# Seven pairs of states per half summed by accumulating DMAs, with a new order of the work

## The chip, the core and the metric

The kernel runs on one core of a Trainium2 chip. The metric is device time in microseconds (us). The engines are TensorE (PE in the profile, its weight loads PEld), VectorE (DVE), ScalarE (ACT), GpSimd (POOL) and SyncE (SP, which here only issues DMAs).

## The reference, cut to what matters

The input is 4096 rows of 1024 numbers in fp32. Three blocks follow each other, each added to the rows: half of a linear layer with ternary weights on the normalised rows, a selective state-space layer, and the linear layer again. Only the middle one matters for the change:

```python
xz = x @ W_in.T;  u, z = split(xz)                 # 2 x 1024 channels
u  = silu(conv_b + sum(conv_w[:, k] * shifted u))  # 4 taps
dt = softplus(dt_r @ W_dt.T + b_dt)                # dt_r, B, C = u @ W_xproj.T
h  = exp(dt * A) * h + dt * B_t * u                # 16 states n per channel, in order of t
y  = sum over n of h[n] * C_t[n] + u * Dskip
out = (y * silu(z)) @ W_out.T
```

The sum in the line of `y` has seventeen terms: one for each of the sixteen states, and the term with `Dskip`.

## The kernel before

**Tiling.** The rows are cut into 16 chunks of 256 rows. In the state-space layer the 1024 channels of a chunk are two halves of 512, so there are 32 halves. A tile of a half is 128 partitions by 4 blocks by 256 rows, 512 KB in fp32.

**One state of one half.** Five streams work on state `n`, from -1 (the `Dskip` term) and 0 to 15.
- `decaying` (ACT, line 911) makes the decays `da`, four instructions.
- `enter` (POOL, lines 934 and 944) makes `h = g * B` in two instructions, and adds what the chunk before left.
- `recur` (DVE, line 969) runs the recurrence in two scans, and `left` (DVE, line 985) multiplies by C: the *product* `p`.
- `summed` (PE, line 1052) transposes a product with the identity into the two PSUM accumulators `y`, eight matrix instructions for a product. That is how the seventeen terms are added up.
- `skipping` (ACT, line 897) makes the term -1.

The product tiles have five buffers, `h` three, the broadcast rows `bc` of B and C six, and the streamed weights five.

**Pairs.** Two terms can be added before PE sees them, so that PE transposes their sum alone. `PAIRED` names states whose product DVE adds to that of the state before (`paired`, line 1002). `SENT` names states for which POOL issues a DMA that accumulates the earlier product onto the later one, both in SBUF (`beside`, line 1020); its source's buffer comes free when it has landed. Before, `SENT` is (1, 5, 9) in every half. `PAIRED` is (7,) in the 28 halves of chunks 1 to 14, (12, 14) in the two halves of the first chunk, and empty in the last. So PE transposes 13, 12 and 14 products in a half of the middle chunks, the first and the last.

**Other work.** Around the states run the linear layers (`ffn`, line 488, with `normed`, `transposed`, and `cut` at 445 and 447, and an accumulating DMA of the bias from DRAM, line 461), the input projection of u (`front`, line 608, and `conv`, 539 to 549), of z (`gates`, line 668, and `kept`, 682 to 687) and the output projection (`back`, line 751, and `mixed`, 722). They stream their weights with DMAs issued by SP (`streamed`), 512 KB each.

**What sets the order.** The instructions of each engine run in an order fixed when the program is built. The class `Streams` holds a clock for each engine and reckons, from durations written into the streams, which stream comes next; constants give the ranks of the streams (`DECAY` to `FFN_C`, `Z`), how long a lower rank is held back for a higher one (`HOLD`), margins on when something counts as ready (`LATE_P` for a product, `LATE_D` for a decay, `LATE_N` and `LATE_X`), and at which recurrence step a piece of the other work may begin (`TRIG`). A DMA of a pair counts as landed `ISSUE` (600 ns) and `ADDED` (9500 ns) after its issue begins, and its transposes may begin 160 ns (`REACH`) later. On the chip only semaphores decide when an instruction may start; the order stays. In `summing` the sum of a pair that goes by DMA is put 3.2 states later in PE's order (`DEFER`).

Of the kernel before, what the change touches and what calls it, by code (L numbers as in the profile page):

```python
# [27 lines left out]

FULL, PASS, TURN = 0.844, 0.449, 0.855
REACH = 160  # L30
ISSUE, ADDED = 600, 9500
SWITCH = 1300

LATE_P, LATE_X, LATE_D, LATE_N = 400, 100, 1700, 1300
PAIRED = (7,)
PAIRED_FIRST = (12, 14)
PAIRED_LAST = ()
TRIG = (-11, -16, 5, 1, -6, -16, 16, -2, 9, 12, 0, -17, 7, -7, -19, -8, -12)
ENTERED = 2
POOLED = ()  # L40
SENT = (1, 5, 9)
DEFER = 2.2, 3.2
Q_SOON = False

DECAY, ENTER, SUM, PREPARE, RECUR, GATE = 5, 0, 0, 0, 4, 1
FFN_A, NORM, U_PART, CONV, DELTA, OUT, FFN_C = 0, 5, 1, 3, 4, 2, 1

HOLD = (1300, 0, 100, 2600)
Z = (5, 7)


class Streams:
# [109 lines left out]
def macaron_mamba_kernel(  # L162
# [169 lines left out]

    def streamed(load, n, ahead, rank):

        queue = []

        def fill():
            for i in range(n):
                yield lambda: 0 if len(queue) < ahead else INF
                w = yield from weights.take()  # L340
                load(i, w)
                queue.append((order.now + 5000, w))

        order.spawn(fill(), rank)
        return queue

    def arrived(queue):
        yield lambda: queue[0][0] if queue else INF
        return queue.pop(0)[1]

    def u_weights(i, w):
# [76 lines left out]
            order.spawn(parts(g, pt, end + REACH), rank)  # L428


    def ffn(c, which, rank, at, tiles=range(TT)):
        ln, rows_, at = yield from stats(c, at, tiles)
        key = which, c

        def split(t):

            xn, begin = yield from normed(c, ln, rows_, t, at)
            hi = yield from his.take()
            lo = yield from los.take()
            ends = []  # L440

            def cut(g, pt, at_):
                part_hi, part_lo = (flat(p_[:, 4 * g : 4 * g + 4, :]) for p_ in (hi, lo))
                end = yield act(512, at_)
                nc.scalar.copy(part_hi, pt)  # L445
                end = yield dve(600, end + REACH)
                nc.vector.tensor_tensor(part_lo, pt, part_hi, ALU.subtract)  # L447
                banks.put(pt, end)
                ends.append(end)
                if len(ends) == NB // 4:  # L450
                    ready["parts", key, t] = end + REACH + LATE_N
                    parts[t] = lo, hi

            order.spawn(biased(t, begin), rank)
            yield from transposed(xn, begin, cut, rank)

        def biased(t, at_):

            yield from when("hbias")
            end = yield pool(ISSUE, at_, False)  # L460
            nc.gpsimd.dma_start(x_tiles[c, t], hbias.to_broadcast([P, D]), accum_op=ALU.add)
            ready["bias", key, t] = end + ADDED

        def residual(t, cols, pf, at_):
            at_ = max(at_, (yield from when("bias", key, t)))
            end = yield dve(660, at_)
            xt = x_tiles[c, t][:, cols]
            nc.vector.scalar_tensor_tensor(xt, pf, hscl, xt, ALU.mult, ALU.add)  # L468
            (ys if (*key, t) == ("a", 0, 1) else banks).put(pf, end)
            ready["ffn", key, t, cols.start] = end  # L470
            if key == ("c", NC - 1):
                yield from give_out(c, t, cols, end)

        parts = {}
        for t in tiles:
            order.spawn(split(t), rank)
        if key == ("a", 0):
            yield from as_weights_come(key, parts, residual, rank)
        for t in tiles if key != ("a", 0) else ():
            begin = yield from when("parts", key, t)  # L480
            lo, hi = parts[t]
            for h in range(2):
                cols = slice(h * OH, (h + 1) * OH)
                pf = yield from banks.take()
                for x in (lo, hi):
                    end = yield pe(8 * OH * PASS, 0, "r")
                    for k in range(NB):
                        nc.tensor.matmul(  # L488
                            pf,
                            x[:, k, :],  # L490
                            wf[:, k, cols],
                            start=(x is lo and k == 0),
                            stop=(x is hi and k == NB - 1),
                        )
                order.spawn(residual(t, cols, pf, end + REACH + LATE_X), rank)
            los.put(lo, end)
            his.put(hi, end)
        lns.put(ln, end if key != ("a", 0) else order.now)
        ends = {}
        for t in tiles:  # L500
            left = yield from when("ffn", key, t, 0)
            right = yield from when("ffn", key, t, OH)
            ends[t] = max(left, right)
        return ends

    def as_weights_come(key, parts, residual, rank):

        for t in range(TT):
            yield from when("parts", key, t)
        groups = {}  # L510
        for h in range(2):
            groups[0, h] = yield from banks.take()
            groups[1, h] = yield from ys.take()
        for k in range(NB):
            yield from when("wf", k)
            end = yield pe(8 * OH * PASS, 0, "r")
            for (t, h), pf in groups.items():
                for i in range(2):
                    nc.tensor.matmul(
                        pf,  # L520
                        parts[t][i][:, k, :],
                        wf[:, k, h * OH : (h + 1) * OH],
                        start=(k == 0 and i == 0),
                        stop=(k == NB - 1 and i == 1),
                    )
        for (t, h), pf in groups.items():
            order.spawn(residual(t, slice(h * OH, (h + 1) * OH), pf, end + REACH), rank)
        for t in range(TT):
            los.put(parts[t][0], end)
            his.put(parts[t][1], end)  # L530
# [4 lines left out]
    def conv(c, blk, pp, at):  # L535
        half, b = divmod(blk, HB)
        ub, rows_ = u[c, half][:, b, :], pp[:, KER - 1 : KER - 1 + T]
        end = yield act(T, at)
        nc.scalar.activation(  # L539
            ub,  # L540
            rows_,
            AF.Identity,
            bias=pr[:, blk, C_CB : C_CB + 1],
            scale=pr[:, blk, C_CW + KER - 1 : C_CW + KER],
        )
        for k in range(KER - 1):
            end = yield dve(391, end + (REACH if k == 0 else 111))
            tap = pr[:, blk, C_CW + k : C_CW + k + 1]
            nc.vector.scalar_tensor_tensor(ub, pp[:, k : k + T], tap, ub, ALU.mult, ALU.add)  # L549
        banks.put(pp, end)  # L550
        done = ready.setdefault(("conv", c, half), [])
        done.append(end)
        if len(done) == HB:
            end = yield act(D, end + REACH, "silu")
            nc.scalar.activation(flat(u[c, half]), flat(u[c, half]), AF.Silu)
            ready["u", c, half] = end + REACH

    def front():
        for c in range(NC):
# [28 lines left out]
            for t in range(TT):  # L588
                xn, at = xns[t]
                yield from transposed(xn, at, keep, NORM)  # L590
                while len(ends) < 2 * (t + 1):
                    yield lambda: ends[2 * t + 1] if len(ends) > 2 * t + 1 else INF

            end = yield pool(190)
            nc.gpsimd.tensor_copy(xT[:, :, PAD - KER + 1 : PAD], halo)  # L595
            at = max(end, ends[-1]) + REACH
            yield U_PART
            for blk in range(NB):
                yield from step(c, 2 + blk // 2)
                if blk % HB == 0:  # L600
                    u[c, blk // HB] = yield from us.take()
                pp = yield from banks.take()
                w = yield from arrived(queue)
                wt = w.rearrange("p (k m) -> p k m", m=P)
# [75 lines left out]
    def kept(c, half, b, pp, at):  # L680
        end = yield act(512, at)
        nc.scalar.copy(sz[c, half][:, :, b * P : (b + 2) * P], pp)
        banks.put(flat(pp), end)
        if b + 2 == HB:
            z = flat(sz[c, half])
            end = yield act(D, end + 125, "silu")
            nc.scalar.activation(z, z, AF.Silu)
            ready["z", c, half] = end + REACH

# [37 lines left out]
    def turned(c, half, yT):  # L727
# [15 lines left out]
                nc.tensor.transpose(pt[:, cols], sz[c, half][:, t, cols], ident)  # L743
            order.spawn(keep(t, pt, end + REACH), OUT)
        szs.put(sz[c, half], end)
        yield lambda: ends[-1] if len(ends) == TT else INF

    def by_w_out(po, yT, w, half, t):
        wt = w.rearrange("p (k m) -> p k m", m=QW)
# [207 lines left out]
    def recur():  # L957
        behind = None
        for c, half, n in items:
# [4 lines left out]
            for j in range(2):  # L964
# [3 lines left out]
                rows_ = flat(h[:, 2 * j : 2 * j + 2, :])  # L968
                nc.vector.tensor_tensor_scan(rows_, flat(da), rows_, 0.0, ALU.mult, ALU.add)  # L969
                decays.put(da, end)  # L970
                ready["step", (2 * c + half) * NST + n] = end
                if behind and j == 0:
                    yield from left(*behind)
                if behind and j == (0 if Q_SOON else 1):
# [38 lines left out]
    def beside(c, half, n):  # L1013
# [4 lines left out]
        if n in SENT:  # L1018
            end = yield pool(ISSUE, at, False)
            nc.gpsimd.dma_start(flat(p), flat(q), accum_op=ALU.add)  # L1020
            end = end + ADDED
        else:
            for j in range(0, HB, 2):
                end = yield pool(1250, at, True)
# [128 lines left out]
```

## Time and profile before

| | us |
|---|---|
| median of 3 runs (2601.02 to 2603.2) | 2602.99 |
| the profiled execution | 2601.62 |
| its span, first to last instruction | 2599.9 |
| PE busy | 2441.9 (94%) |
| PE weight loads busy | 2093.8 (81%) |
| DVE busy | 2314.4 (89%) |
| ACT busy | 1925.1 (74%) |
| POOL busy | 1896.4 (73%) |

A busy time is the sum of one engine's instructions in the profiled execution. Matrix instructions overlap each other, so PE's time per instruction is better read from the distance between starts. The DMA queues are told apart by who builds the transfers: q1 carries what SP issues, q0 what POOL issues (96 pairs and 64 biases).

### The profile page before, as it was taken

The page shows a single profiled execution, that of the slowest core. Times are in us where ns is not written, and L with a number is a line of the kernel's source. Part 1 is how long each engine was busy: PE and PEld are TensorE (multiplying, and loading weights), DVE is VectorE, ACT ScalarE, POOL GpSimd, SP SyncE. Part 2 cuts the span into 40 slices and gives each one's busy share as a digit, 9 for nine tenths or more (in the row PEclk, how much of TensorE's full clock was granted, in tenths as well). Part 3 has the DMA queues.
Part 4 walks back from the last instruction along what each step waited for, and adds up shares of the span by engine and source line. Part 5 has one row for each costly group of instructions (what it writes and reads, how often), then busy time and mean ns, then how long its engine had stood idle before and what let it go on. Part 6 is the DMA issues. An engine that isn't in the chain of part 4 may idle for free. (4 is left out here: it accounts for less than half of the span.)

```text
span 2599.9 us, 39031 instructions
## 1 busy us (share of the span) xinstructions
PE 2441.9 (94%) x13058; PEld 2093.8 (81%) x13058; DVE 2314.4 (89%) x2468; ACT 1925.1 (74%) x4056; POOL 1896.4 (73%) x2041
## 2 busy tenths in 40 slices
PE   5988899999999999999999999999999999999787
PEld 4776787888888888888888888888888888887676
DVE  4588998999999899999989999899999989999795
ACT  3678677687877868787786868878687786877563
POOL 0467867778787787878778686877878677787683
PEclk9989999999999999999999999999999999999888
DMA  4546556766766666666566765665675567666462
GB/s 165 156 129 187 175 158 178 198 180 195 197 173 166 196 185 199 186 182 188 167 190 195 203 178 161 189 195 168 196 207 168 167 193 191 188 192 173 149 165 65
DMA packets 232369, 461.03 MB, mean 177 GB/s; under 512 B 20708, under 2 KB 87396, under 8 KB 232168
## 3 DMA queue, kind: packets, MB, share of 16 engines
q1 hardware_dynamic: 209128, 374.65, 43.2%
q0 software_dynamic: 23040, 83.90, 18.6%
q8 instruction: 103, 1.69, 0.3%
q14 instruction: 98, 0.80, 0.1%
HBM read 390.82 MB, written 17.31 MB: 157 GB/s over the span
## 5 line engine op out<-in xcount | busy, mean ns | idle before, releaser
L934 POOL TENSOR_TENSOR h<-u,bc 128x512 f32<-128x512 f32 x1024 | 1339.5, 1335 | 444.9 <-ACT da L911 153.2
L969 DVE TENSOR_TENSOR_SCAN h<-da,h 128x512 f32<-128x512 f32 x1024 | 1215.4, 1206 | 78.8 <-ACT da L911 54.9
L911 ACT ACTIVATE da<-dt,pr 128x255 f32<-128x255 f32 x2048 | 953.1, 474 | 409.2 <-DVE h L969 373.7
L985 DVE TENSOR_TENSOR p<-h,bc 128x1024 f32<-128x1024 f32 x512 | 672.5, 1314 | 0.1
L1052 PE MATMUL y<-ident,p 128*128 128x128 f32 x3328 | 438.5, 278 | 69.0 <-DVE p L985 35.0
L668 PE MATMUL bank<-weight,xT 128*128 128x256 f32 x2048 | 479.5, 383 | 14.5 <-DMA weight<-in_w_in 9.6
L608 PE MATMUL bank<-xT,weight 128*128 128x259 f32 x2048 | 475.4, 385 | 14.3 <-POOL xT L595 5.2
L1052 PEld LDWEIGHTS y<-ident,p 128*128 128x128 f32 x3328 | 387.0, 143 | 124.1 <-DVE p L985 48.5
L751 PE MATMUL bank<-weight,u 128*128 128x256 f32 x2016 | 452.6, 381 | 7.7 <-DMA weight<-in_w_out 7.1
L608 PEld LDWEIGHTS bank<-xT,weight 128*128 128x128 f32 x2048 | 382.1, 191 | 77.3 <-issue 8.9
L668 PEld LDWEIGHTS bank<-weight,xT 128*128 128x128 f32 x2048 | 378.6, 192 | 65.9 <-ACT da L911 9.8
L751 PEld LDWEIGHTS bank<-weight,u 128*128 128x128 f32 x2016 | 381.4, 191 | 60.4 <-issue 5.6
L944 POOL TENSOR_TENSOR h<-h,over 128x4 f32<-128x4 f32 x512 | 272.0, 531 | 36.1
L488 PE MATMUL bank<-wf,lo 128*128 128x512 f32 x976 | 258.3, 407 | 5.3 <-DVE lo L447 3.8
L488 PE MATMUL bank<-wf,hi 128*128 128x512 f32 x976 | 243.3, 391 | 0.0
L488 PEld LDWEIGHTS bank<-wf,lo 128*128 128x128 f32 x976 | 181.5, 191 | 49.7 <-DVE x L468 7.6
L549 DVE SCALAR_TENSOR_TENSOR u<-bank,pr,u 128x256 f32<-128x256 f32 x384 | 176.8, 469 | 43.4 <-ACT u L539 40.9
L488 PEld LDWEIGHTS bank<-wf,hi 128*128 128x128 f32 x976 | 182.8, 189 | 37.6
L417 PE MATMUL bank<-ident,tmp 128*128 128x128 f32 x756 | 116.0, 288 | 38.1 <-ACT tmp L401 26.6
L386 ACT ACTIVATE tmp<-x,ln 128x1024 f32<-128x1024 f32 x96 | 110.1, 1146 | 37.8 <-POOL ln L384 37.6
L417 PEld LDWEIGHTS bank<-ident,tmp 128*128 128x128 f32 x756 | 95.5, 149 | 51.6 <-ACT tmp L401 28.8
L468 DVE SCALAR_TENSOR_TENSOR x<-bank,hscl,x 128x512 f32<-128x512 f32 x124 | 91.6, 739 | 43.4 <-PE bank L488 41.9
(99 smaller groups left out, 1936.2 us busy)
## 6 DMA issues: line engine op xcount, KB each, us to landing
bc<-bcd SPq DMA_DIRECT2D x512, 256.0 KB, 4.1
weight<-in_w_in SPq DMA_DIRECT2D x128, 512.0 KB, 4.8
weight<-in_w_in SPq DMA_DIRECT2D x256, 256.0 KB, 5.3
weight<-in_w_out SPq DMA_DIRECT2D x128, 512.0 KB, 6.1
p<-p POOLq DMA_DIRECT2D x96, 512.0 KB, 5.8
x<-hbias POOLq DMA_DIRECT2D x64, 512.0 KB, 8.1
x<-in_x SPq DMA_DIRECT2D x32, 512.0 KB, 4.7
out<-x SPq DMA_DIRECT2D x30, 512.0 KB, 4.7
```

The source lines that it names most:

```text
L417: nc.tensor.matmul(pt[:, j * P : (j + 1) * P], xn[:, k * P : (k + 1) * P], ident, start=(j == 0), stop=(j == 3), is_transpose=True, skip_g ...
L488: nc.tensor.matmul(pf, x[:, k, :], wf[:, k, cols], start=(x is lo and k == 0), stop=(x is hi and k == NB - 1),)
L549: nc.vector.scalar_tensor_tensor(ub, pp[:, k : k + T], tap, ub, ALU.mult, ALU.add)
L608: nc.tensor.matmul(pp[:, : KER - 1 + T], wt[:, k, :], xT[:, k, PAD - KER + 1 : PAD + T], start=(k == 0), stop=(k == NB - 1),)
L668: nc.tensor.matmul(pp[:, t, :], xT[:, k, PAD + t * P : PAD + (t + 1) * P], wt[:, :, i, :], start=(k == 0 and t == 0), stop=(k == NB - 1), ...
L751: nc.tensor.matmul(po[:, t, :], yT[:, b, t * P : (t + 1) * P], wt[:, b, :], start=(half == 0 and t == 0 and b == 0), stop=(half == 1 and b ...
L911: nc.scalar.activation(da[:, i, 1:], dt[c, half][:, b, 1:], AF.Exp, scale=a_neg[:, half * HB + b, n : n + 1],)
L934: nc.gpsimd.tensor_tensor(h[:, some, :], u[c, half][:, some, :], bc[:, 0:1, :].to_broadcast([P, ENTERED, T]), ALU.mult,)
L944: nc.gpsimd.tensor_tensor(h[:, :, 0], h[:, :, 0], over[c, half][:, :, n], ALU.add)
L969: nc.vector.tensor_tensor_scan(rows_, flat(da), rows_, 0.0, ALU.mult, ALU.add)
L985: nc.vector.tensor_tensor(p, h, bc[:, 1:2, :].to_broadcast([P, HB, T]), ALU.mult)
L1052: nc.tensor.matmul(y[t][:, b * P : (b + 1) * P], p[:, b, t * P : (t + 1) * P], ident, start=(first and b == 0), stop=(final and b == HB - ...
```

## The change

`SENT` becomes (0, 2, 4, 6, 8, 10, 12) in every half, and the three `PAIRED` lists become empty. So in each half the terms (-1, 0), (1, 2) to (11, 12) are added by seven accumulating DMAs, and PE transposes ten tiles: seven sums, and the products 13, 14 and 15. A pair's DMA counts as landed `SUMMED` (7500 ns) after the issue, in place of 9500. Several waits of the reckoning name the stage that they need (each part of `cut`, each block of `conv`, each part of `kept`), where they counted stages done. A recurrence step counts as done for `TRIG` after its second scan, no longer after its first. The ranks, margins and triggers have other values. No other instruction of the engines is added or taken away.

```diff
-ISSUE, ADDED = 600, 9500
+ISSUE, ADDED, SUMMED = 600, 9500, 7500
-LATE_P, LATE_X, LATE_D, LATE_N = 400, 100, 1700, 1300
-PAIRED = (7,)
-PAIRED_FIRST = (12, 14)
+LATE_P, LATE_X, LATE_D, LATE_N = 1600, 300, 0, 900
+PAIRED = ()
+PAIRED_FIRST = ()
 PAIRED_LAST = ()
-TRIG = (-11, -16, 5, 1, -6, -16, 16, -2, 9, 12, 0, -17, 7, -7, -19, -8, -12)
+TRIG = (-7, -26, -11, 12, -9, 17, -9, -24, -1, 37, -40, -9, -4, -1, -2, -14, 44)
-SENT = (1, 5, 9)
+SENT = (0, 2, 4, 6, 8, 10, 12)
-DECAY, ENTER, SUM, PREPARE, RECUR, GATE = 5, 0, 0, 0, 4, 1
-FFN_A, NORM, U_PART, CONV, DELTA, OUT, FFN_C = 0, 5, 1, 3, 4, 2, 1
-HOLD = (1300, 0, 100, 2600)
-Z = (5, 7)
+DECAY, ENTER, SUM, PREPARE, RECUR, GATE = 9, 4, 6, 1, 9, 6
+FFN_A, NORM, U_PART, CONV, DELTA, OUT, FFN_C = 0, 7, 3, 1, 0, 7, 5
+HOLD = (500, 100, 100, 0)
+Z = (8, 7)
...
     def streamed(load, n, ahead, rank):
-        queue = []
+        queue, gone = [], []
         def fill():
             for i in range(n):
-                yield lambda: 0 if len(queue) < ahead else INF
+                if i >= ahead:
+                    yield lambda: gone[i - ahead] if len(gone) > i - ahead else INF
...
+    def cuts(key, t):
+        for g in range(NB // 4):
+            yield from when("cut", key, t, g)
...
-                ends.append(end)
-                if len(ends) == NB // 4:
-                    ready["parts", key, t] = end + REACH + LATE_N
-                    parts[t] = lo, hi
+                ready["cut", key, t, g] = end + REACH + LATE_N
...
-        done = ready.setdefault(("conv", c, half), [])
-        done.append(end)
-        if len(done) == HB:
-            end = yield act(D, end + REACH, "silu")
-            nc.scalar.activation(flat(u[c, half]), flat(u[c, half]), AF.Silu)
-            ready["u", c, half] = end + REACH
+        ready["conv", c, blk] = end + REACH
+    def activated(c, half):
+        for blk in range(half * HB, (half + 1) * HB):
+            end = yield from when("conv", c, blk)
+        end = yield act(D, end, "silu")
+        nc.scalar.activation(flat(u[c, half]), flat(u[c, half]), AF.Silu)
+        ready["u", c, half] = end + REACH
...
-                ready["step", (2 * c + half) * NST + n] = end
+                if j:
+                    ready["step", (2 * c + half) * NST + n] = end
...
             nc.gpsimd.dma_start(flat(p), flat(q), accum_op=ALU.add)
-            end = end + ADDED
+            end = end + SUMMED
```

More of the change, by code (lines that the diff above doesn't have):

```diff
@@ L344, in streamed @@
         order.spawn(fill(), rank)
-        return queue
+        return queue, gone
     def arrived(queue):
-        yield lambda: queue[0][0] if queue else INF
+        queue, gone = queue
+        at = yield lambda: queue[0][0] if queue else INF
+        gone.append(at)
         return queue.pop(0)[1]
@@ L439, in split @@
             lo = yield from los.take()
-            ends = []
+            parts[t] = lo, hi
             def cut(g, pt, at_):
@@ L479, in ffn @@
         for t in tiles if key != ("a", 0) else ():
-            begin = yield from when("parts", key, t)
+            yield from cuts(key, t)
             lo, hi = parts[t]
@@ L508, in as_weights_come @@
         for t in range(TT):
-            yield from when("parts", key, t)
+            yield from cuts(key, t)
         groups = {}
@@ L590, in front @@
                 yield from transposed(xn, at, keep, NORM)
-                while len(ends) < 2 * (t + 1):
-                    yield lambda: ends[2 * t + 1] if len(ends) > 2 * t + 1 else INF
+                yield lambda: max(ends) if len(ends) == NB // 4 * (t + 1) else INF
             end = yield pool(190)
             nc.gpsimd.tensor_copy(xT[:, :, PAD - KER + 1 : PAD], halo)
-            at = max(end, ends[-1]) + REACH
+            at = max(end, max(ends)) + REACH
             yield U_PART
@@ L601, in front @@
                     u[c, blk // HB] = yield from us.take()
+                    order.spawn(activated(c, blk // HB), CONV)
                 pp = yield from banks.take()
@@ L683, in kept @@
         banks.put(flat(pp), end)
+        ready["kept", c, half, b] = end + 125
         if b + 2 == HB:
+            for b in range(0, HB, 2):
+                end = yield from when("kept", c, half, b)
             z = flat(sz[c, half])
-            end = yield act(D, end + 125, "silu")
+            end = yield act(D, end, "silu")
             nc.scalar.activation(z, z, AF.Silu)
@@ L745, in turned @@
         szs.put(sz[c, half], end)
-        yield lambda: ends[-1] if len(ends) == TT else INF
+        yield lambda: max(ends) if len(ends) == TT else INF
     def by_w_out(po, yT, w, half, t):
```

## The prediction, made before the change had been run

> **What bounds the kernel now.** I read the page's busy times first, then the stages, to see whether those shares hold throughout.
>
> ```profile
> PE 2441.9 (94%) x13058; PEld 2093.8 (81%) x13058; DVE 2314.4 (89%) x2468; ACT 1925.1 (74%) x4056; POOL 1896.4 (73%) x2041
> ```
>
> ```profile
> core 0: us, PE busy (x) PEld busy (x) DVE busy (x) ACT busy (x) POOL busy (x), PEclk, DMA share, GB/s
> 0.00:130.00 130.00, 97.27 (x430) 80.21 (x431) 66.35 (x93) 64.74 (x114) 34.54 (x54) 0.93 0.51 161
> 610.00:930.00 320.00, 312.97 (x1704) 269.68 (x1704) 298.12 (x318) 246.23 (x523) 251.38 (x265) 1.00 0.66 188
> 2500.00:2600.00 100.00, 80.27 (x392) 66.78 (x390) 67.61 (x68) 38.46 (x89) 49.21 (x52) 0.89 0.45 123
> ```
>
> The middle of the run, 290 to 2210 us, looks like the second stage: PE 98% busy, DVE 93%, ACT 77%, POOL 79%. Only the ends have much empty PE time. Chunks follow each other every 151 us: the sixteen halo copies of line 595 start from 48.3 to 2312.1, (2312.1 - 48.3) / 15 = 150.9, so a half takes 75.5 us. Ends of matrix instructions are modelled, so I checked PE's load by starts in the timeline:
>
> ```profile
> 1268.97 1.04 PE L1052 MATMUL y<-ident,p 128*128 128x128 f32 x8
> 1269.85 3.62 PE L668 MATMUL bank<-weight,xT 128*128 128x256 f32 x16
> 1273.30 1.04 PE L608 MATMUL bank<-xT,weight 128*128 128x259 f32 x4
> ```
>
> The eight transposes of a product are busy for 1.04 us but hold PE for 0.88 (to the next start); the sixteen of L668 hold it 3.45, or 0.216 each. In such distances, the three projections (6144 instructions, 0.216) hold PE 1327 us, the linear layers (2048, about 0.24 each: 8 of L488 busy 1.98 to 2.19 us) some 490, transposes (4352, 0.11) 479, the small products (512, 0.216) 111: together 2407 of 2600. So PE is nearly full by either measure, and is the bound; DVE is second, close behind.
>
> The Trainium skill (Perfetto Trace Analysis, Identifying the Most-Contended Engine) says that matmul busy time judges TensorE's headroom badly and weight-load busy time well. By that rule PE stands at 81%, DVE at 89% is the most contended, and the gain would be at most DVE's 53.7 us below, about 2549. The start distances speak for the matmul row here.
>
> **The change part by part.** The rows that price it:
>
> ```profile
> L969 DVE TENSOR_TENSOR_SCAN h<-da,h 128x512 f32<-128x512 f32 x1024 | 1215.4, 1206 | 78.8 <-ACT da L911 54.9
> ...
> L668 PE MATMUL bank<-weight,xT 128*128 128x256 f32 x2048 | 479.5, 383 | 14.5 <-DMA weight<-in_w_in 9.6
> ...
> L751 PE MATMUL bank<-weight,u 128*128 128x256 f32 x2016 | 452.6, 381 | 7.7 <-DMA weight<-in_w_out 7.1
> L1052 PE MATMUL y<-ident,p 128*128 128x128 f32 x3328 | 438.5, 278 | 69.0 <-DVE p L985 35.0
> ...
> L1002 DVE TENSOR_TENSOR p<-p,p 128x1024 f32<-128x1024 f32 x32 | 53.7, 1678 | 0.0
> ...
> q0 software_dynamic: 23040, 83.90, 18.6%
> ...
> p<-p POOLq DMA_DIRECT2D x96, 512.0 KB, 5.8
> ```
>
> ```profile
> L1020 POOL DMA_DIRECT2D p<-p x96: 860/881/948, 119.0 to 2539.3; - x96
> DMA to landing us min/median/max: 4.6/5.8/10.7
> ```
>
> ```profile
> PE y L1052 <- DVE p L1002: 23.6, 16, 5.0
> ...
> DVE h L969 <- POOL h L944: 23.9, 27, 3.1
> ```
>
> (A group's line ends with its idle time and what ended it; the last fence holds waits: us in total, times, longest; the one before, all issues of a pair's transfer and its landings.)
>
> *PE loses transposes.* 3328 / 8 = 416 products now; ten in each of 32 halves after, 320. The 96 fewer are three in each of 28 middle halves, two in each of the first two, four in each of the last two. At 0.88 us they free 84 us. The 12 of the first and last chunk (11 us) lie in the stages where PE is 75 to 80% busy; I count them at nothing, as other waits end last there. The 84 products of the middle lie where PE is full: 84 x 0.88, -74 us. Bounds: -84, and nothing if DVE or a transfer takes over.
>
> *DVE loses 32 adds*, 53.7 us. They free nothing more while PE is the bound. But DVE must keep up. In the 1920 us of the middle lie about 25 halves: DVE falls from 1780 to 1780 - 25 x 1.68 = 1738, PE from 1869 to 1869 - 76 x 0.88 = 1802; at PE's present fill the stretch would last 1851 us, with DVE's empty time down from 140 to 113. If all the 27 us of lost slack become waits of PE, it costs 27; if none, nothing. I take 10: the largest waits of DVE are for PE and ACT (ACT da 54.9, PE bank L488 41.9), not DVE holding PE up.
>
> *POOL gets 128 more issues*, 128 x 0.891 = 114 us, or 3.6 us in each half. POOL is empty for some 16 of a half's 75.5 us (79% busy), so they fit. What is queued behind an issue is `enter` of the next state, and behind that DVE's scan. Today DVE waits for POOL's `h` 27 times in 1024 scans, 23.9 us in all. Bounds: nothing, and 114 us if every issue delays a scan. I take 5, near the row.
>
> *The wait moves from an add to a landing.* PE waits today 23.6 us for the adds of L1002, which go. In PE's queue 224 sums, not 96, then stand behind a landing, and everything PE does is queued behind them. In the list of waits no line has PE waiting for a `p` transfer. The order allows 600 + 7500 + 160 = 8.26 us from issue to transposes (10.26 before); the median landing is 5.8, the longest 10.7. Bounds: -24 us; and 2.4 us (10.7 - 8.26) for one in ten of 224, +54, less 24, so +30. I take 0, since the median is well inside.
>
> *The DMA engines.* 160 transfers of q0 take 18.6% of 2600 us, 3.0 us each over all sixteen engines. 128 more add 387 us, taking q0 to q14 together from 62% to 77%. Weights are what they can hold up: PE waits 9.6 + 7.1 = 16.7 us for them now (L668 and L751). A pair's transfer is in flight 96 x 5.8 / 2600 = 21% of the time, afterwards 224 x 5.8 / 2555 = 51%; scaled with that the waits become 40 us. Bounds 0 and +23; I take 12, as not all of today's waits come from pairs.
>
> The skill's SBUF page (SBUF — State Buffer, SBUF: two separate sides) speaks against sending by POOL: DVE instructions that hold the port shared with GpSimd keep it from writing descriptors. If every added issue waited for one product of 1.2 us, that would be 154 us, on the landings. The row of issues, 860 to 948 ns, shows no such wait in the instruction itself, though the landings spread by 6 us.
>
> *The buffers.* A state takes 75.5 / 16 = 4.7 us. With 8 us from issue to landing, the earlier product stays some 15 us and the later some 13, every 9.4 us: three buffers of five on average. No cost.
>
> *The new order.* No row prices it. In the middle PE waits for 2% of the time, about 45 us over the run, and that is all a better order can win; for a loss, the second stage above (312.97 of 320 us) against the least full one of the middle, 290 to 610 us (309.15), differs by 3.8 in 320, 31 over a run. So -45 to +31, taken as 0. The named waits change what the reckoning knows, and no instruction.
>
> **The sum.** -74 + 10 + 5 + 0 + 12 = -47 us. On the profiled execution: 2601.6 - 47 = 2554.6; the median of the runs is 1.4 higher: 2556.
>
> **The rivals.**
> - *Landings come late, and PE's queue stands.* Place: the 224 sums in PE's order. An accumulating transfer needs all engines for 3.0 us; with 77% of their time taken, one more transfer ahead of it makes a usual landing 5.8 + 3.0 = 8.8 us, 0.54 beyond what the order allows. Price: 224 x 0.54 = 121 us if it hits all, 60 if it hits half. It decides from 47 / 224 = 0.21 us of mean lateness. For it: transfers in flight half of the time, an allowance cut by 2 us, landings up to 10.7 already. Against it: no PE wait for 96 of them today. With half of them: 2556 + 60 = 2616.
> - *DVE becomes the bound.* Its 93% leaves only 5.5 us in a half; if order and port keep it there, the middle shrinks only by DVE's 42 us less POOL's delays and the weights' (5 + 12): -25, about 2578. For it: the busy shares lie close. Against it: DVE's waits are mostly for PE's banks, which come earlier.
> - *All of it comes through.* PE's 84 us and the 24 us of waits for adds, DMA and POOL hidden: 2603 - 108 = 2495. For it: POOL and the DMA engines have room. Against it: the ends of the run do not shrink with PE.
> - *The pairs do not come about.* Then PE would still transpose 416 products and the time would be 2603, but for the order. `summing` and `beside` read `SENT` alone, so I see little chance.
>
> **How the numbers follow.** A measurement of this kernel can tell about 0.2%, 5 us, from no change. Chances: the forecast (2525 to 2570) 0.45; DVE as the bound (2570 to 2597) 0.18; all of it (below 2525) 0.12; late landings or an order that loses as much (above 2608) 0.20; no pairs, or gain and loss equal (2598 to 2608) 0.05. So faster 0.75, same 0.05, slower 0.20. The range reaches from 2512, within the third case, to 2625, just beyond half of the landings being late; I leave about 0.08 below and 0.10 above. The likeliest sign's own range is 2512 to 2597.
>
> **What would show it.** The page after should have 2560 transposes at L1052's successor, about 100 us less busy there (96 x 1.04); no DVE add of `p<-p`; 224 issues of `p<-p`, 200 us; DMA busy near 77%. If the forecast holds, chunks come every 148 us, the middle keeps PE at 97% and DVE near 94%, and the median landing stays below 7 us. Late landings would show as PE (or PEld) `y` waiting for DMA `p<-p`, by more than 47 us in all, with PE below 95%. DVE as the bound would show DVE above 95% in the middle and PE waiting for DVE. I am wrong in kind if PE's empty time in the middle grows by more than the 74 us that it lost in work.

## The result, and the profile after

The changed kernel takes 2620.5 us (median of 4 runs, 2619.3 to 2621.7) against 2603.1 before: 1.0069 times as long, 95% interval 1.0051 to 1.0086. The prediction was 2556, faster. Its profiled run is 2619.6 us, span 2617.8.

First the page of the changed kernel: busy times, the group of the z projection (line 674, before 668), the transposes, and the pairs' issues.

```profile
PE 2384.6 (91%) x12290; PEld 2036.1 (78%) x12290; DVE 2297.3 (88%) x2436; ACT 1910.2 (73%) x4055; POOL 1997.0 (76%) x2169
...
q0 software_dynamic: 41472, 151.01, 31.7%
...
L674 PE MATMUL bank<-weight,xT 128*128 128x256 f32 x2048 | 505.9, 400 | 87.7 <-DMA weight<-in_w_in 84.4
...
L1062 PE MATMUL y<-ident,p 128*128 128x128 f32 x2560 | 331.2, 278 | 32.3 <-DMA p<-p 22.0
...
L1030 POOL DMA_DIRECT2D p<-p x224 | 202.7, 905 | 15.9 <-issue 11.5
...
p<-p POOLq DMA_DIRECT2D x224, 512.0 KB, 6.2
```

Everything that was meant to go has gone: 768 transposes less (107 us of busy time), no add on DVE, 224 issues. Yet PE is busy for a smaller share of a longer span, and one line has grown: waits for the z weights, from 9.6 to 84.4 us. The list of waits has its count, and a second wait that was 5.8 us before (ACT for rows of x):

```profile
PE bank L674 <- DMA weight<-in_w_in: 84.4, 16, 7.3
...
ACT tmp L385 <- DMA x<-in_x: 47.3, 15, 4.0
```

Of the sixteen waits, fourteen are 5.4 to 7.3 us long, one in each of fourteen chunks. Here is the one near 1165 us, on PE and then on SP, the queue that issues the weights (start, length, instruction, idle time before it in brackets):

```profile
1156.13 5.45 PE L674 MATMUL bank<-weight,xT 128*128 128x256 f32 x24
1161.42 1.04 PE L1062 MATMUL y<-ident,p 128*128 128x128 f32 x8
1162.29 1.89 PE L674 MATMUL bank<-weight,xT 128*128 128x256 f32 x8
1169.83 8.32 PE L674 MATMUL bank<-weight,xT 128*128 128x256 f32 x24 [5.65 <-DMA weight<-in_w_in]
1177.98 1.04 PE L420 MATMUL bank<-ident,tmp 128*128 128x128 f32 x8
```

```profile
1150.69 0.42 SPq L224 DMA_DIRECT2D x<-in_x  x1
1154.37 0.32 SPq L890 DMA_DIRECT2D bc<-bcd  x1
1154.78 0.87 SPq L772 DMA_DIRECT2D out<-x  x1
1160.25 0.33 SPq L224 DMA_DIRECT2D x<-in_x  x1
1160.69 0.37 SPq L772 DMA_DIRECT2D out<-x  x1
1161.15 1.68 SPq L363 DMA_DIRECT2D weight<-in_w_in  x2
```

The second load of x, at 1160.25, writes the buffer that the store at 1154.78 reads, and SP waits for that store to land (in SP's waits: x for out, 59.7 us in 13 times). The z weights stand behind it on SP, are issued at 1161.15, and are wanted at 1164, when PE has used up the two weight tiles that were loaded earlier. Before, the same wait existed (51.7 us, 13 times), and the same loads stood behind it in the same order. Here it is in the kernel before, on SP and on PE:

```profile
1305.27 0.38 SPq L763 DMA_DIRECT2D out<-x  x1
1309.73 0.33 SPq L224 DMA_DIRECT2D x<-in_x  x1
1310.17 0.37 SPq L763 DMA_DIRECT2D out<-x  x1
1311.54 0.32 SPq L881 DMA_DIRECT2D bc<-bcd  x1
1311.95 2.05 SPq L360 DMA_DIRECT2D weight<-in_w_in  x4
```

```profile
1311.30 7.07 PE L668 MATMUL bank<-weight,xT 128*128 128x256 f32 x32
1319.32 1.97 PE L668 MATMUL bank<-weight,xT 128*128 128x256 f32 x8 [0.95 <-ACT da L911]
```

There PE begins the z projection after SP's wait has ended, 0.65 us before the weights are issued (1311.30 and 1311.95). In the changed order it begins while SP still waits, 5.0 us before they are issued (1156.13 and 1161.15).

The stall also costs after it has ended: 24 matrix instructions that hold PE 5.2 us at full rate (0.216 each) hold it 8.15 (1169.83 to 1177.98). The stages around it show why, in the clock (the number before the DMA share):

```profile
core 0: us, PE busy (x) PEld busy (x) DVE busy (x) ACT busy (x) POOL busy (x), PEclk, DMA share, GB/s
1165.00:1170.00 5.00, 0.17 (x1) 0.20 (x2) 3.85 (x4) 4.97 (x13) 3.27 (x7) 0.89 1.06 264
1170.00:1177.00 7.00, 7.00 (x20) 5.68 (x21) 3.19 (x3) 3.31 (x6) 6.25 (x7) 0.59 1.08 365
```

In the middle of the run the granted clock is half its full rate for 6.8 us at each such stall (3.4 us at the first). From the mean clock, the time at half rate in the whole run is 2 x (1 - 0.963) x 2617.8 = 194 us, against 2 x (1 - 0.981) x 2599.9 = 99 us before. This is the "half-clock time" of the expectations below. Half of the difference, 48 us, would be lost work if PE worked all through it. But there the clock falls 0.5 to 3.5 us before PE goes on, so part of that time is the stall itself: the 2048 instructions of the z projection are busy 505.9 us in place of 479.5, and 26 us is the loss that shows. The DMA engines are full at that moment (share 1.06), with a pair's transfer issued at 1160.85 among the loads. The z weights' loads of 256 KB land 7.5 us after their issue (median), against 5.3 before. So two causes were possible: the queue, or the pairs' traffic.

### The profile page after: what moved, and what is told of

Same layout as the page of the kernel before. It is cut to its first block, busy times and chain, and to the rows that moved or that the text cites. A ratio compares the mean times of both kernels' runs of the same rounds, so it can differ in the third digit from the quotient of the medians.

```text
span 2617.8 us, 37697 instructions
## 1 busy us (share of the span) xinstructions
PE 2384.6 (91%) x12290; PEld 2036.1 (78%) x12290; DVE 2297.3 (88%) x2436; ACT 1910.2 (73%) x4055; POOL 1997.0 (76%) x2169
## 3 DMA queue, kind: packets, MB, share of 16 engines
q1 hardware_dynamic: 209128, 374.65, 43.3%
q0 software_dynamic: 41472, 151.01, 31.7%
## 5 line engine op out<-in xcount | busy, mean ns | idle before, releaser
L943 POOL TENSOR_TENSOR h<-u,bc 128x512 f32<-128x512 f32 x1024 | 1366.7, 1376 | 334.8 <-DVE u L867 147.3
L995 DVE TENSOR_TENSOR p<-h,bc 128x1024 f32<-128x1024 f32 x512 | 706.6, 1380 | 2.0 <-PE y L1062 1.6
L674 PE MATMUL bank<-weight,xT 128*128 128x256 f32 x2048 | 505.9, 400 | 87.7 <-DMA weight<-in_w_in 84.4
L674 PEld LDWEIGHTS bank<-weight,xT 128*128 128x128 f32 x2048 | 400.2, 202 | 151.8 <-ACT da L920 82.5
L1062 PE MATMUL y<-ident,p 128*128 128x128 f32 x2560 | 331.2, 278 | 32.3 <-DMA p<-p 22.0
L1062 PEld LDWEIGHTS y<-ident,p 128*128 128x128 f32 x2560 | 298.2, 144 | 64.3 <-DVE p L995 14.3
L953 POOL TENSOR_TENSOR h<-h,over 128x4 f32<-128x4 f32 x512 | 309.3, 604 | 33.3
L1030 POOL DMA_DIRECT2D p<-p x224 | 202.7, 905 | 15.9 <-issue 11.5
L387 POOL TENSOR_SCALAR ln<-ln 128x1 f32<-128x1 f32 x96 | 50.6, 527 | 159.6 <-ACT tmp L385 159.6
L385 ACT ACTIVATE tmp<-x 128x1024 f32<-128x1024 f32 x96 | 100.5, 1047 | 91.6 <-DMA x<-in_x 47.3
```

The lines of the kernel that those rows point to most:

```text
L674: nc.tensor.matmul(pp[:, t, :], xT[:, k, PAD + t * P : PAD + (t + 1) * P], wt[:, :, i, :], start=(k == 0 and t == 0), stop=(k == NB - 1), ...
L943: nc.gpsimd.tensor_tensor(h[:, some, :], u[c, half][:, some, :], bc[:, 0:1, :].to_broadcast([P, ENTERED, T]), ALU.mult,)
L953: nc.gpsimd.tensor_tensor(h[:, :, 0], h[:, :, 0], over[c, half][:, :, n], ALU.add)
L995: nc.vector.tensor_tensor(p, h, bc[:, 1:2, :].to_broadcast([P, HB, T]), ALU.mult)
L1062: nc.tensor.matmul(y[t][:, b * P : (b + 1) * P], p[:, b, t * P : (t + 1) * P], ident, start=(first and b == 0), stop=(final and b == HB - ...
```

## The experiments

The theories have letters in the expectations: Q is SP's queue, T the traffic, C that these loads cost as much in any order, D that DVE sets the pace, P that PE does. All differences are against the changed kernel's 2620.5 us unless another is named. The order of PE, DVE, ACT and POOL is that of the changed kernel, except in e3, e4 and e11 (new orders) and e15 (the order before); e6, e9, e14, e16 and e17 repeat some instructions in place.

**Less traffic.**

```diff
-            nc.gpsimd.dma_start(flat(p), flat(q), accum_op=ALU.add)
+            nc.gpsimd.dma_start(flat(p)[:, :P], flat(q)[:, :P], accum_op=ALU.add)
```

> The changed kernel with the same order on every engine, but each pair's DMA adds only the first 128 of the 1024 columns, so seven eighths of each pair's sum are left out and the pairs' traffic falls from 117 MB to 15 MB. Theory Q (SP's queue: in each chunk a load of x waits for a store of out to land, and the z weights, queued behind it on SP, are issued too late for PE): the late issue stays, only the landing is quicker; PE's waits for in_w_in at the z projection fall from 84 us to 40 to 70, time 2570 to 2605. Rival T (traffic: the pairs fill the DMA engines and so the weights land late): the waits fall below 20, half-clock time from 195 us to about 100, time 2510 to 2545.

Measured: 2552.2 us, 68 less. The waits fell to 37.9 us in 14 times, just below Q's 40 to 70 and far from T's 20; the half-clock time fell to 133 us and the time lay between both ranges. The stalls did not go: they shrank below 4 us each.

```profile
PE bank L674 <- DMA weight<-in_w_in: 37.9, 14, 3.8
```

**No wait for the store.**

```diff
-        nc.sync.dma_start(out[rows_, cols], x_tiles[c, t][:, cols])
+        nc.sync.dma_start(out[rows_, cols], wf[:, 0, cols].bitcast(F32))
```

> The changed kernel with the same order on every engine, but the stores of out read a constant tile in place of x (for all chunks; the rows that are written are not the result), so that no load of x has to wait for a store; all bytes are moved as before. Theory Q: SP issues the z weights some 4.5 us earlier in each chunk; PE's waits for in_w_in at the z projection fall from 84 us below 25, the half-clock time from 195 us to about 100, time 2510 to 2550. Rival T (traffic): the waits stay above 60, time within 15 us of 2620.

Measured: 2558.9 us, 62 less, with all the traffic. Waits 41.2 us, half-clock time 137 us. T's condition fell; Q's time was 9 us too low at its upper end, and Q had the waits below 25 us and the half-clock time near 100. The wait on SP is thus not the whole of the stall.

**Both away.**

> As e2_store_elsewhere, and each pair's DMA adds only 128 of the 1024 columns: both suspects of the stall are away in the same order. If the stall needed both, little is left to gain: 2525 to 2550, with PE's waits for in_w_in below 20 us. If the two are separate costs that add (61 and 68 us), 2490 to 2505.

Measured: 2516.4 us, with 9.4 us of waits for weights. That is 104 less than 2620.5, beyond the range for "needed both", short of the sum of 130. So either cure alone shortens one and the same stall, and each has something left for the other: queue and traffic both lengthen it.

**The two halves of the change alone, and the reckoning's waits alone.** e3 is the kernel before with only `SENT`, `PAIRED` and `SUMMED` changed; e4 is the changed kernel with the old `SENT` and `PAIRED`; e11 is the changed code with all constants of before. In these three the reckoning makes a new order.

> The kernel before with only the pairs changed: SENT of seven states, no PAIRED, SUMMED 7500; ranks, margins, triggers and the reckoning's waits stay as before (the order is reckoned anew from them). Theory Q (the new ranks and triggers put the loads in a bad place, the pairs themselves gain): no stall over 5 us per chunk, weights' waits on PE below 45 us, time 2540 to 2580. Rival T (traffic): waits for weights over 60 us, time 2600 to 2650.

> The changed kernel with SENT and PAIRED as before: new ranks, margins, triggers and waits, the old pairs. Theory Q: the stall in SP's queue comes back in most chunks, with 74 us more work of PE: 2650 to 2700, if the anew reckoned order keeps the collision. Rival T: the weights land in time again, PE's waits for them below 30 us, time 2590 to 2620.

> The kernel before with its own pairs, ranks, margins, triggers and 9500 ns, and of the change only the reckoning's waits for named stages and the recurrence step counted after its second scan. The instructions are those of before, their order is reckoned anew. If the waits are neutral, as the prediction took them: 2590 to 2615. If the constants are fitted to one reckoning and any other order loses, as in the two runs with one half of the change each: 2650 to 2760.

Measured: 2759.3 us (1.061 times before, 1.0585 to 1.0628), 2748.6 (1.057, 1.055 to 1.0585) and 2712.0 (1.042, 1.040 to 1.044). In e3 waits for the z weights are 36.6 us, in e4 11.2, in e11 6.5, so neither Q nor T explains them, and the times of e3 and e4 lie above both ranges. e11 is the telling one: the instructions of before, in another order by the same constants, cost 109 us (the order also adds 30 loads of activation tables on ACT, 193 against 163). Each of these three changes of the reckoning's inputs lost 4 to 6% under constants that were kept; that the constants are fitted to one set of inputs is the likely reason, and no run with a new fit shows it. PE's largest waits there are others, 62.1 us for products (e3), 103.0 for ACT's `tmp` (e4) and 62.8 for DVE's adds (e11); what brings them about was not traced.

**SP's order mended by moving the load of x.** In e5 the second load of x is issued 3 us later by the reckoning, which puts it behind two tiles of z weights (two loads each) and one load of W_out; in e8 2 us later, behind the first tile of z weights only.

```diff
+    def loaded(c, t, at): yield lambda: at; load_x(c, t)
...
-                load_x(c, t)
+                order.spawn(loaded(c, t, order.now + 3000 * t), FFN_A)   # e8: 2000
```

> The changed kernel, complete, with the same order on PE, DVE, ACT and POOL; only on SP the second load of x of each chunk is issued 3 us later by the reckoning, that is behind the two loads of z weights that it stood before. Theory Q: the z weights no longer stand behind the wait for the store; PE's waits for in_w_in fall from 84 us below 45 and the half-clock time to about 130 us, as where the store read elsewhere: 2550 to 2570, faster than both kernels. Rival C (any order of these loads collides, since the burst of loads stays): 2600 to 2625.

> The changed kernel, complete, same order on PE, DVE, ACT and POOL; on SP the second load of x of each chunk moves behind only the first load of z weights (2 us later by the reckoning, not 3), so that it is issued when the store has landed, as before, and the z weights some 4 us earlier. Theory Q (two urgent loads, one queue): PE's waits for in_w_in fall below 50 us, ACT's waits for x stay near 50 us, half-clock time near 140 us: 2550 to 2575. Rival C (any order of these loads costs as much, since they share the same moment): 2600 or more.

Measured: e5 2675.6 us, 1.028 times before: a miss, and slower than both. e8 2596.8, 0.998 times before (0.997 to 0.999), between the ranges of Q and C. The waits of e5:

```profile
ACT tmp L385 <- DMA x<-in_x: 153.6, 15, 12.2
...
PE bank L420 <- ACT tmp L404: 140.2, 17, 13.3
```

PE's waits for z weights did fall, to 19.9 us, but now the rows of x came late. ACT's statistics waited for them, and PE waited for ACT. Both loads are urgent at this moment; changing places moves the stall. In e8 both waits remained in part (53.0 us for weights, 87.0 us for x).

e6 and e7 used e5 as their base before that was known:

> As e5_x_behind, but PE transposes the sums of states 2, 6 and 10 twice in each half (the second time adds them again, so these sums count double): 96 groups of eight transposes, as many as the pairs took from PE, come back, and nothing else moves. If PE is the bound in the middle (the term of the prediction), 74 to 84 us more than e5_x_behind: 2625 to 2650. If another engine or the DMAs bound it, less than 40 more.

> As e5_x_behind, but each pair's DMA adds only 128 of the 1024 columns (the rest of the sum is left out), same order. What is left of the pairs' traffic as a cost where SP's queue is mended. Theory Q with the prediction's term for weights: 10 to 25 us less than e5_x_behind. Rival T (traffic is the larger part of it): 40 us less or more.

Measured: e6 2691.1 us, 15 more than e5; e7 2610.9, 65 less. With x late, little follows from e6 for PE. In e7 ACT's waits for x are 99.0 us, against 153.6 in e5: a wait behind a load again shrinks, and does not go, when the pairs' transfers are small. The 65 us are what T foretold here (40 or more), not Q (10 to 25): where a load is late, the traffic is a large part of the price.

**The store sooner.** The remedy that is left is to make the wait short. The store of a chunk's first tile stood until both tiles were done.

```diff
-            if key == ("c", NC - 1):
+            if which == "c":
                 yield from give_out(c, t, cols, end)
...
-                yield from give_out(c, t, slice(0, D), ends[t])
+                yield lambda: ends[t] + REACH + 1
```

> The changed kernel, complete, same order on PE, DVE, ACT and POOL; each tile of out is stored in two halves of its columns, each as soon as its last sum is done, where it was stored whole when both tiles of the chunk were done. So the store that the load of x waits for leaves SP some 10 us earlier. Theory Q: the wait of SP is gone; PE's waits for in_w_in fall from 84 to about 40 us, half-clock time to about 135 us, 2550 to 2570, as in e2_store_elsewhere: faster than both kernels. Rival C (the burst of loads costs as much however SP issues it): 2590 to 2625.

Measured: 2533.5 us (5 runs, 2530.1 to 2536.1), 0.9737 times before, 0.9723 to 0.9750; 87 less than the changed kernel and better than expected. All traffic and all work are there. SP's queue around the same place:

```profile
1110.27 0.34 SPq L772 DMA_DIRECT2D out<-x  x1
...
1115.41 0.36 SPq L772 DMA_DIRECT2D out<-x  x1
...
1122.69 0.34 SPq L772 DMA_DIRECT2D out<-x  x1
1124.98 0.32 SPq L890 DMA_DIRECT2D bc<-bcd  x1
1125.39 0.88 SPq L224 DMA_DIRECT2D x<-in_x  x1
1126.72 0.71 SPq L772 DMA_DIRECT2D out<-x  x1
1127.48 1.14 SPq L363 DMA_DIRECT2D weight<-in_w_in  x2
```

```profile
PE bank L674 <- DMA weight<-in_w_in: 12.2, 12, 5.2
```

The two halves of the first tile leave at 1110.27 and 1115.41, so the load of x at 1125.39 waits for nothing. The z weights follow it by 2.1 us and PE waits 12.2 us for them in all. In the middle (290 to 2210 us) the clock is never halved, against 12 times in the changed kernel.

How the edits act can be read from the traces. PE begins the z projection with two tiles in place, which with the transposes between them last it 8.0 us (7.1 before); the third tile is the one that was held up. Medians over the third to the fourteenth chunk, in us:

| | third tile's issue after PE begins | issue to landing | PE's gap before it |
|---|---|---|---|
| before | 0.65 | 6.6 | 0.4 |
| changed | 5.1 | 8.6 | 5.8 |
| e1, small pairs | 4.1 | 6.6 | 3.0 |
| e2, no wait | 2.4 | 7.3 | 1.7 |
| e12, store sooner | 0.7 | 7.3 | 0.3 |

The gap is what issue and landing together exceed those 8 us by. Against before, the issue comes 4.5 us later and the landing takes 2.0 longer, while the work in hand is 0.9 longer. Between e2 and e12 the landing is equal and the issue 1.6 us sooner. So the stall is shown: PE begins the z projection earlier than SP can issue its weights, and the pairs' traffic lengthens what follows. With that traffic whole, the loss goes when the store leaves sooner.

**The same wait in the order before.**

> The kernel before in its own order, but the stores of out read a constant tile (the rows written are not the result), so that no load of x waits for a store. Theory Q (in the order before nothing urgent stood behind that wait): 2590 to 2605, within half a per cent. If the wait costs the same in any order: 2530 to 2560.

(The edit is that of e2.) Measured: 2594.4 us, 0.9975 times before (0.9961 to 0.9990), 7 us. There the wait is nearly free, since PE begins the z projection only when it is over; it is dear only in the new order.

**Is PE's work what sets the pace?** e9, e14 and e16 give the 96 groups of transposes back to PE, on e2, on e10 and on e12.

```diff
-                for b in range(HB):
+                for b in list(range(HB)) * (2 if n in (2, 6, 10) else 1):
```

> As e2_store_elsewhere (stores of out read a constant tile), and PE transposes the sums of states 2, 6 and 10 twice in each half (they count double): the 96 groups that the pairs took from PE come back in the same order. If the prediction's term for PE is right, 74 to 84 us more than the 2559 of e2_store_elsewhere: 2630 to 2645. If PE has slack there or another engine bounds it, less than 45 more: below 2604.

> As e10_elsewhere_small (stores of out read a constant tile, each pair's DMA adds 128 of 1024 columns), and PE transposes the sums of states 2, 6 and 10 twice (they count double): the 96 groups come back where the loads are in time. If PE's work is the bound there, as the prediction had it: 74 to 84 us more than 2516, so 2590 to 2600. If PE has slack there too: below 2560.

> As e12_out_halves, and PE transposes the sums of states 2, 6 and 10 twice in each half (they count double): 96 groups, 84 us of PE. Theory D (DVE, with the shared port, sets the pace): 15 to 25 us more than 2533. Theory P (PE sets it, as the prediction had it): 74 to 84 more, 2607 to 2617.

Measured: 2580.3, 2532.3 and 2550.0 us: 21, 16 and 17 more than their bases, for 84 us of work (two runs each, which differ by 3 to 11 us). All three lie where the expectations put them if PE has room. In e16 the row of the transposes grows by 83 us (329.7 to 412.8). Net over PE, 24 of these run under the tails of other matrix instructions, 41 fill what was empty time (171 to 130 us), and 18 lengthen the span. e17 gives DVE about as much:

```diff
-        nc.vector.tensor_tensor(p, h, bc[:, 1:2, :]...)
+        for _ in range(2 if n in (5, 11) else 1): nc.vector.tensor_tensor(p, h, bc[:, 1:2, :]...)
```

> As e12_out_halves, and DVE multiplies the products of states 5 and 11 a second time in each half (the same result): 64 more products of about 1.3 us, 83 us of DVE. Theory D: 60 to 85 us more than 2533, 2593 to 2618. Theory P: DVE has 5% empty, and less than 30 more.

Measured: 2586.2 us, 53 more than e12. The group of products grew from 692.9 us to 782.5, by 90:

```profile
L995 DVE TENSOR_TENSOR p<-h,bc 128x1024 f32<-128x1024 f32 x576 | 782.5, 1358 | 3.8 <-PE y L1062 1.6
```

So 59% of added DVE work shows in the time (53 / 90), and 20% of added PE work (17 / 84). D's range began at 60 us, P's ended at 30; the result is nearer D, which had e16 right too (15 to 25 us). In the middle stage PE and DVE stand like this, first e12, then e16 (with PE's work back):

```profile
610.00:930.00 320.00, 313.61 (x1659) 268.32 (x1658) 303.35 (x327) 254.31 (x547) 269.99 (x293) 1.00 0.82 221
```

```profile
610.00:930.00 320.00, 317.54 (x1743) 275.88 (x1742) 300.28 (x323) 252.08 (x541) 267.31 (x289) 1.00 0.81 220
```

PE goes from 98.0 to 99.2% busy, while DVE falls from 95 to 94%.

## Why the prediction was wrong, step by step

- **The weights' term failed: +12 us.** It scaled today's 16.7 us of waits by the pairs' time in flight, with +23 as the upper end. They became 90 us (84.4 and 5.8 at the z and the output projection), 73 more, and the halved clock added 26: about 100. The share of the DMA engines was not wrong in kind (43.3 + 31.7 = 75%, against 77 foretold). What the step left out is SP's queue. The prediction asked who stands behind POOL's issues and in PE's queue; it did not ask how soon PE would want the weights that stand behind the load of x on SP, though SP's waits of before showed 51.7 us there. The new order moved PE's z projection 4.5 us ahead of that queue, and the traffic lengthened the landing by 2.0; the prediction took order and traffic as two separate terms, and they met in one stall.
- **The new order's term failed: 0, between -45 and +31.** Its bounds came from PE's empty time and from the difference of two stages of one order. PE's empty time in the middle is 51 us (1920 - 1869), more than the 45 that the lower bound was read as, and e11, the old instructions in another order, is +109. The diff showed that nearly every rank and trigger changed; a bound from the stages of one well-fitted order says nothing of others.
- **A price was missing: a stall's aftermath.** The wait of 5.65 us cost about 8.6: 5.65, and the 3 us by which 24 instructions took longer at half clock. The Trainium skill states it (TensorE: Matmul & The Clock Gate, HAM oscillation — how this bites in real kernels): idle gaps beyond about 3.4 us put the array back to half rate. The runs agree in part. After stalls of 5.4 to 6.1 us the clock falls in all 12 chunks of the middle; with stalls of 1.8 to 3.8 us (e1) it falls in five, and there a gap of 3.77 us left it whole while one of 2.80 halved it.
- **PE's term, -74, was mis-sized, and DVE's, 0, too.** Taken back on a fixed order, PE's 84 us are worth 16 to 21 us, DVE's work 59% of its length: the 53.7 us of adds would be about 32 (an estimate from e17). Adding work to a fixed order isn't the exact reverse of taking it out before the order is made, but it shows that PE at 98% busy was not the bound the prediction made of it; the rival in which DVE becomes the bound was nearer. So was the rule that the prediction quoted from the Trainium skill (Perfetto Trace Analysis, Identifying the Most-Contended Engine) and set aside, that matmul busy time judges TensorE's headroom badly; but e12's 2533.5 us lies below the 2549 that the prediction drew from it. Of e12's gain of 68 us (2601.1 to 2533.5) some 17 and 32 are PE's and DVE's by these rates (an estimate); what the rest is was not settled.
- **A reading was off:** 151 us per chunk is a mean over unequal distances; from the fourth copy of line 595 on they are 153.4 to 155.2 us. No term rests on it by more than a rounding.
- **Right:** POOL's 128 issues fitted (905 ns each, and DVE's waits for `h` 25.2 us against 23.9). The pairs' landings stayed short (6.2 us, below the 7 that were named), and PE's waits for them are 22.0 us, less than the 23.6 of the adds that they replaced. So the rival that ended slower had the sign and the wrong place: late landings, but of weights, not of pairs.

## What to carry to other kernels

Where a change moves loads in time, write down the queue of the engine that issues them, and for every wait in it what stands behind and when that is wanted; a wait that cost next to nothing (7 us) in one order stalled the fullest engine once per chunk in another. If a buffer's next load waits for a store, issue that store as early as its data allows: here this turned a loss of 0.7% into a gain of 2.6%. Where an order is reckoned from fitted constants, half of a change can't be judged alone by switching the other half off, and an engine's share of busy time doesn't say what its work is worth; add work to it and measure.

## What the runs showed of the hardware that was not expected

Only the price of stalls. The stalls of the changed kernel took 72 us of waits more than in e12 (84.4 less 12.2) and another 26 us through the clock (the z projection's instructions are busy 505.9 against 480.0 us), and the two kernels differ by 87 us, less than the sum; why less is not settled. And when a stall halves the clock: in each of the eighteen traces the halvings begin on a fixed grid of 3.41 us and last one or more of its steps. In the middle of the run (290 to 2210 us) every step in which PE was idle for more than 2.01 us was followed by one at half rate, and of the steps with less than 1.9 us of idle time only three were, all in e3. So in these runs a gap of 2.04 us halved the clock where it fell into one step (e2, near 1145 us), and one of 3.77 us did not where the grid cut it in two (e1, near 845 us).
